# Projecting the queries of the last block by seven half-size products, in a kernel for gated attention with a mixture of experts

## The chip, the cores and the metric

The kernel runs on one core of a Trainium2 chip. The metric is the device time of one execution in microseconds (us), the median of several runs. A profile is one further execution, taken with the hardware profiler. The engines are TensorE (PE in the profile), VectorE (DVE), ScalarE (ACT), GpSimd (POOL) and SyncE (SP, which only issues transfers). PEld is TensorE's loading of weights. ACT, POOL and SP issue transfers (DMAs) from their own queues of instructions, in order: a transfer that must wait holds what is behind it on that engine.

## The reference

Two sequences of 2048 tokens, 512 wide, all in float32:

```
xn = layernorm(x)
z  = layernorm(xn) * gamma + beta
q, k, v = z @ qkv[:, :512], z @ qkv[:, 512:1024], z @ qkv[:, 1024:]
s  = softmax(causal(q @ k.T / sqrt(512))) @ v @ o_proj + xn
# mixture of experts on xn: 8 experts of 352 hidden units, the best 2 of each token
scores = xn @ gate_w.T + gate_b + bias
comb   = softmax over the 2 best scores, spread over the experts
h = silu(einsum('td,ehd->teh', xn, w1) + b1)
y = einsum('teh,edh->ted', h, w2) + b2
g = silu(einsum('td,te->t', y, comb))          # summed over the experts
out = x + s * g
```

## The kernel before

The work has four stages. **Projection** (to about 247 us): the 32 tiles of 128 tokens form 8 blocks of 512. The query and key weights are folded into one matrix `wqk`, the value and output weights into `wvo`, so each block has only queries (`wqk` on the left, the block's normalised rows `kT` on the right) and values (`kT` on the left, `wvo` on the right) to be made; `kT` itself serves as keys. **Routing** runs beside the last part of it: ranks, positions and lists of tokens for each expert, mostly on VectorE. **Experts** follow (`up`, `turn_h`, `join_h`, `down` for each tile of 128 sorted tokens), and then **attention**, with the gating and the output.

A block's queries are either four *units* (a unit is four products of 128x128 by 128x512, gathered in one PSUM bank, then copied by ScalarE and stored) or the seven products of the Strassen-Winograd scheme, each of four 128x128 by 128x256 products. `one_product(i, k)` makes product `k` of `items[i]`, where an item is a block's queries or its values. It needs sums of the weights (`wsums`, made once) and of the block's keys (`ksums`, by `key_sums`). The products 1, 2, 3, 4, 6 and 7 gather in the banks a, b and c; ScalarE copies bank_a into bank_b after product 1 and bank_b into bank_c after product 6, so that the later products add to what is there. Product 5 has bank_d and is added to two of the four results by VectorE, later: `with_fifth` puts the addition into `deferred`, and `add_due` emits it. Finished results go to `unstored`, and `store` issues their transfers; from block `LATE` = 5 on these stand on ScalarE's queue.

`SEVEN` = 7: the blocks 0 to 6 are made by seven products, the last block, 7, by eight units. `chain_of_products` gives the order of products, with two units of block 7 (the entries `None`) in the last item. `pieces` is a generator that yields after about every 7/4 products, or after a unit; the rest of the units follow at its end. The main loop, and then `route`, pull pieces and put other work between them; the order of the program is the order on each engine, as it is written out by hand. `route` emits its arithmetic between pieces; after its last `yield` come the list of tokens `toki`, six gathers on GpSimd, and the rest of the arithmetic (`ge`, `b1sel`, `share`). The last six pieces are pulled by the loop over `experts_step(-5)` to `experts_step(-1)`.

The memory is shared over time. `arena` holds the sums in six `areas` during the projection (area 0 the query weights' sums, 1 the value weights', 2 to 4 the sums of keys in turn, 5 a result) and later the second weights of the experts, `w2`, 1536 columns each, so that the experts 0 and 1 lie over area 0 and half of area 1, and 2 and 3 over the rest of 1 and area 2. `load_w2(e)` loads one expert's, in the order of `w2_left`. The pool `kp` has four buffers, in turn for the blocks' `kT` and, late, for results (`late_outs`). When the projection is over, its pools are closed, and `keep` (a mask, filled by GpSimd) and `w1s` (sums of the first weights, made by VectorE) take their memory.

Of the kernel before, what the change touches and what calls it, by code (L numbers as in the profile page):

```python
# [10 lines left out]
F32 = mybir.dt.float32  # L11
# [4 lines left out]
ALU = mybir.AluOpType  # L16
# [4 lines left out]
P = 128  # L21
# [5 lines left out]
def gated_attention_moe(  # L27
# [28 lines left out]
    nc = tc.nc  # L56
    B, S, D = x.shape
    E, _, H = w1_t.shape
# [6 lines left out]
    ND = D // P  # L65
# [79 lines left out]
    kp = right(stage_a, name="kp", bufs=BT)  # L145
# [54 lines left out]
    raw = w1p.tile([P, E * ND * H], F32, name="raw", tag="w1")  # L200
# [191 lines left out]
    def add_due(wait=2):  # L392
        while deferred and deferred[0][0] + wait <= made[0]:
            _, f, args = deferred.pop(0)
            f(*args)
# [40 lines left out]
            ratio.rearrange("p t o -> p o t").to_broadcast([P, E, BT]), ALU.mult,  # L436
        )

    def unit(b, u):

        kT = kts[b]
        po = banks[(u + 3) % ND]
        r = u % ND
        for c in range(ND):
            if u < ND:
                nc.tensor.matmul(
                    po, lhsT=wqk[:, c, ts(r, P)], rhs=kT[:, c, :],
                    start=(c == 0), stop=(c == ND - 1),
                )
            else:  # L450
                nc.tensor.matmul(
                    po, lhsT=kT[:, c, ts(r, P)], rhs=wvo[:, c, :],
                    start=(c == 0), stop=(c == ND - 1),
                )
        o = stg.tile([P, TB], F32, name=f"j_{b}_{u}", tag="stg")
        nc.scalar.copy(o, po)
        nc.scalar.dma_start(out=(qt_d if u < ND else v_d)[b][:, r, :], in_=o)
# [12 lines left out]
    def four(i):  # L470
        return areas[i].rearrange("p (k c d) -> p k c d", k=4, c=ND // 2)
# [3 lines left out]
        wsums[name] = four("qv".index(name))  # L475
        lhs_sums(wsums[name], w)

    def key_sums(b):

        assert all(k != b for _, _, _, k in pending)  # L480
        s = ksums[b] = four(2 + b % 3)
        b11, b12, b21, b22 = (
            kts[b][:, 2 * i : 2 * i + 2, ts(j, HD)] for i in range(2) for j in range(2)
        )
        nc.gpsimd.tensor_tensor(s[:, 0], b12, b11, ALU.subtract)
        nc.gpsimd.tensor_tensor(s[:, 1], b22, s[:, 0], ALU.subtract)
        nc.gpsimd.tensor_tensor(s[:, 2], b22, b12, ALU.subtract)
        nc.gpsimd.tensor_tensor(s[:, 3], b21, s[:, 1], ALU.subtract)

    items = [(b, of_q) for b in range(SEVEN) for of_q in (True, False)]
    FIFTH = {}

    def chain_of_products():
        yield from ((0, k) for k in (1, 5, 2, 6))
        for i in range(len(items) - 1):
            for j, k in (1, 1), (0, 3), (0, 7), (1, 5), (0, 4), (1, 2), (1, 6):
                yield i + j, k  # L500
        for k in (None, 3, 7, None, 4):
            yield len(items) - 1, k

    def one_product(i, k):

        b, of_q = items[i]
        w, s, t = wqk if of_q else wvo, wsums["q" if of_q else "v"], ksums.get(b)
        a11, a12, a21, a22 = (w[:, 2 * j : 2 * j + 2, ts(i, HD)] for i in range(2) for j in range(2))
        b11, b12, b21, b22 = (
            kts[b][:, 2 * i : 2 * i + 2, ts(j, HD)] for i in range(2) for j in range(2)  # L510
        )
        if k == 2 and i in (first_late, first_late + 2):
            late_outs.append(kp.tile([P, ND * D], F32, name=f"so_{i}", tag="kT"))
        outs = (
            raw[:, ts(i % NRAW, ND * D)] if i < first_late
            else areas[5] if i == first_late + 1
            else late_outs[int(i == first_late + 2)] if k in (2, 3, 7, 4) else raw[:, : ND * D]
        ).rearrange("p (g r d) -> p g r d", g=2, r=2)
        bank_a, bank_b, bank_c, bank_d = banks

        def multiply(bank, x, y, start=False):
            ps = bank.rearrange("p (r d) -> p r d", r=2)
            lhs, rhs = (x, y) if of_q else (y, x)
            for r in range(2):
                for c in range(2):
                    nc.tensor.matmul(
                        ps[:, r, :], lhsT=lhs[:, c, ts(r, P)], rhs=rhs[:, c, :],
                        start=(start and r + c == 0), stop=(c == 1), skip_group_check=True,
                    )

        def place(i, j):
            g, c = (i, j) if of_q else (j, i)
            return outs[:, g, :, ts(c, HD)]

        def whole(bank):
            return bank.rearrange("p (r d) -> p r d", r=2)

        def with_fifth(out, bank):
            nc.scalar.copy(out, whole(bank))
            deferred.append((made[0], nc.vector.tensor_tensor, (out, out, whole(FIFTH[i]), ALU.add)))  # L540

        if k == 1:
            multiply(bank_a, a11, b11, start=True)
            if i == 0:
                nc.scalar.copy(bank_b, bank_a)
        elif k == 5:
            multiply(bank_d, s[:, 0], t[:, 0], start=True)
            FIFTH[i] = stg.tile([P, TB], F32, name=f"p5_{i}", tag="stg")
            nc.scalar.copy(FIFTH[i], bank_d)
        elif k == 2:  # L550
            multiply(bank_a, a12, b21)
            nc.scalar.copy(place(0, 0), whole(bank_a))
        elif k == 6:
            multiply(bank_b, s[:, 1], t[:, 1])
            nc.scalar.copy(bank_c, bank_b)
        elif k == 3:
            multiply(bank_b, s[:, 3], b22)
            with_fifth(place(0, 1), bank_b)
            if i + 1 < len(items):
                nc.scalar.copy(bank_b, bank_a)  # L560
            while unstored:
                store(*unstored.pop(0))
        elif k == 7:
            multiply(bank_c, s[:, 2], t[:, 2])
            with_fifth(place(1, 1), bank_c)
            del FIFTH[i]
        else:
            multiply(bank_c, a22, t[:, 3])
            nc.scalar.copy(place(1, 0), whole(bank_c))
            queue = nc.sync if b < LATE else nc.scalar  # L570
            unstored.extend(((qt_d if of_q else v_d)[b], g, outs[:, g], queue) for g in range(2))

    def store(dst, g, src, queue):

        queue.dma_start(out=dst[:, 2 * g : 2 * g + 2, :], in_=src)
# [3 lines left out]
    def route():  # L579

        with ExitStack() as rt:
# [209 lines left out]
            nc.vector.tensor_copy(toki, tokf)  # L791
            for i in range(FIRST):
                gather(i)


            GS = [P, NJ, E]
# [113 lines left out]
    def pieces():  # L910

        n = 0
        for i, k in chain_of_products():
            if k is None:
                unit(*units.pop(next(j for j, (b, _) in enumerate(units) if b == SEVEN)))
                yield
                continue
            made[0] = n
            add_due()
            one_product(i, k)  # L920
            scale_next()
            n += 1
            if n * 4 // 7 > (n - 1) * 4 // 7:
                units.pop(0)
                yield
        while units:
            add_due(0)
            unit(*units.pop(0))
            while unstored:
                store(*unstored.pop(0))  # L930
            yield

    def sum_keys(i):
# [20 lines left out]
    def load_w2(e):  # L954
        nc.sync.dma_start(
            out=w2[:, e, : NH - 1, :],
            in_=w2_t[e, :full_rows, :].rearrange("(c p) d -> p c d", p=P),
        )
        nc.sync.dma_start(out=w2[:HL, e, NH - 1, :], in_=w2_t[e, full_rows:, :])
        nc.sync.dma_start(out=w2[HL : HL + 1, e, NH - 1, :], in_=b2[e : e + 1, :])  # L960
# [7 lines left out]
    def gather(i):  # L968
        xs = xsp.tile([P, ZW], U16, name=f"xs_{i}", tag="xs")
        nc.gpsimd.indirect_dma_start(  # L970
            out=xs, out_offset=None, in_=zu_d,
            in_offset=bass.IndirectOffsetOnAxis(ap=toki[:, order[i] : order[i] + 1], axis=0),
        )
        xss[i] = xs

    w2_left = [4, 5, 6, 7, 0, 1, 2, 3]
    done = LAST
    W2_FROM = 2 * ND * (SEVEN - 1) + 4
    for n in route():
        for _ in range(n):  # L980
            next(projected)
            done += 1
            for f, args in between.pop(done, []):
                f(*args)
            sum_keys(done)
            if done >= W2_FROM:
                load_w2(w2_left.pop(0))


# [407 lines left out]
    for i in range(-5, 0):  # L1397
        experts_step(i)
        for _ in range(min(2, len(units) - 1) if i < -1 else len(units)):
            next(projected)  # L1400
            if w2_left:
                load_w2(w2_left.pop(0))
    while w2_left:
        load_w2(w2_left.pop(0))
    stage_a.close()
    yp = st.enter_context(tc.tile_pool(name="yp", bufs=2))
    sm = right(att, name="sm2", bufs=4)
# [533 lines left out]
```

## Time and profile before

| what | value |
|---|---|
| time, median of 3 runs | 1008.62 us (1008.32 to 1014.06) |
| the profiled execution | 1007.83 us, span 1006.0 us |
| granted TensorE clock | 1.00 |
| instructions | 13431 |
| DMA | 207.96 MB, mean 207 GB/s |

The span is from the first to the last instruction of the profiled execution; the execution's time has a little more around it. In rows of the timeline the columns are: start, duration (both us), engine, line of the kernel, operation, output and inputs, shapes, how often, and in brackets the engine's idle time before it and what ended it. `ACTq` or `SPq` is an engine's queue that issues a transfer; its duration includes what it waited for. In the list of waits: who waited, for whom, us in total, how often, the longest. TensorE works on float32 in two passes, so a product of 128x128 by 128x512 is two rows of `128x512`. Rows of PE have an end that is modelled and overlaps the next start; the distance from start to start is the time that one takes.

### The profile page before, as it was taken

How to read it: one execution, taken by the hardware profiler on the slowest of the kernel's cores; microseconds unless marked ns; L12 is line 12 of the kernel's file. 1: busy time of each engine (PE TensorE's matmuls, PEld its weight loads, DVE VectorE, ACT ScalarE, POOL GpSimd, SP SyncE). 2: the span in 40 equal slices, each digit the busy share in tenths (PEclk: the TensorE clock that was granted, in tenths of full speed). 3: DMA queues.
4: the chain of work that ended last, by engine and by line, in shares of the span. 5: the costliest groups of instructions: out<-in, count | busy, mean ns of one | idle time of the engine just before them, and what ended most of it. 6: DMA issues, size and time to landing. Idle time of an engine off the chain costs nothing. (4 is left out here: it accounts for less than half of the span.)

```text
span 1006.0 us, 13431 instructions
## 1 busy us (share of the span) xinstructions
PE 999.9 (99%) x3924; PEld 665.3 (66%) x3924; DVE 716.9 (71%) x1396; ACT 403.2 (40%) x804; POOL 483.3 (48%) x475
## 2 busy tenths in 40 slices
PE   9999999999999999999999999999999999999998
PEld 5888888874567767766753448677675544447577
DVE  6996746897887777677744579668576556878667
ACT  3344445322444454444445112232335535442241
POOL 4474564004644454444332165254557776764272
PEclk9999999999999999999999999999999999999999
DMA  8689996978999999999999576274677768753361
GB/s 293 193 264 293 329 286 258 349 249 240 202 227 220 211 208 221 217 200 222 216 218 242 164 193 147 78 206 104 183 199 239 225 200 240 207 141 86 92 165 42
DMA packets 296647, 207.96 MB, mean 207 GB/s; under 512 B 230776, under 2 KB 243832, under 8 KB 296576
## 3 DMA queue, kind: packets, MB, share of 16 engines
q1 hardware_dynamic: 282432, 163.56, 63.2%
q0 software_dynamic: 10400, 34.63, 12.5%
q10 hardware_dynamic: 3744, 8.91, 2.4%
q8 instruction: 34, 0.56, 0.2%
q14 instruction: 37, 0.30, 0.1%
HBM read 92.35 MB, written 60.03 MB: 151 GB/s over the span
## 5 line engine op out<-in xcount | busy, mean ns | idle before, releaser
L1195 PE MATMUL py<-arena,ht 128*128 (+3 forms) x396 | 176.7, 593 | 0.0
L1307 PE MATMUL ps<-k,q 128*128 128x512 f32 (+3 forms) x416 | 143.0, 495 | 0.3 <-PEq L1455 0.3
L1495 POOL COPY pu<-pT 128x1024 uint16<-128x1024 uint16 (+2 forms) x74 | 82.5, 1146 | 118.1 <-ACT pT L1485 59.1
L1166 POOL COPY hu<-h 128x704 uint16<-128x704 uint16 x66 | 61.9, 956 | 155.8 <-issue 121.7
L1195 PEld LDWEIGHTS py<-arena,ht 128*128 128x128 f32 (+3 forms) x396 | 71.8, 185 | 80.7 <-issue 76.9
L1307 PEld LDWEIGHTS ps<-k,q 128*128 128x128 f32 x416 | 74.7, 190 | 67.1 <-issue 56.5
L970 POOL DMA_INDIRECT xs<-zu_d,toki x66 | 77.6, 1176 | 70.2 <-DVE toki L791 55.6
L1181 ACT ACTIVATE ht<-ht,b1sel 128x128 f32<-128x128 f32 (+3 forms) x216 | 67.9, 380 | 88.1 <-DVE ht L1175 88.1
L1145 DVE TENSOR_TENSOR h<-p,h 128x176 f32<-128x176 f32 x182 | 55.5, 337 | 60.7 <-PE p L1138 57.2
L1678 POOL DMA_INDIRECT yg<-y_d,posi x64 | 67.4, 1053 | 36.9 <-DVE yg L1689 21.9
L1535 PE MATMUL po<-v,pT 128*128 128x512 f32 x152 | 67.9, 592 | 0.0
L347 POOL COPY zu<-z 128x1024 uint16<-128x1024 uint16 x32 | 39.9, 1245 | 55.7 <-DVE z L332 55.7
L1517 DVE COPY pT<-puT 128x1024 uint16<-128x1024 uint16 (+2 forms) x74 | 54.1, 759 | 8.8 <-DMA puT<-pu 8.6
L1485 ACT ACTIVATE pT<-pT,nm 128x1024 f32<-128x1024 f32 x14 | 16.1, 1148 | 110.3 <-DVE nm L1395 72.0
L1203 ACT COPY y<-py 128x512 f32<-128x512 f32 x55 | 32.2, 585 | 62.3 <-PE py L1195 48.4
L1485 ACT ACTIVATE pT<-ps,nm 128x512 f32<-128x512 f32 (+3 forms) x52 | 30.1, 581 | 62.5 <-DVE nm L1395 38.8
L1365 DVE TENSOR_TENSOR pT<-p,pT 128x512 f32<-128x512 f32 x49 | 32.9, 687 | 25.8 <-PE p L1359 22.1
L1535 PEld LDWEIGHTS po<-v,pT 128*128 128x128 f32 x152 | 28.6, 190 | 31.9 <-issue 30.1
L1707 POOL TENSOR_TENSOR o<-o,yg 128x512 f32<-128x512 f32 x30 | 42.0, 1398 | 14.3 <-DVE o L1699 14.1
L1699 DVE SCALAR_TENSOR_TENSOR o<-xo,xscale,o 128x512 f32<-128x512 f32 x30 | 25.9, 871 | 30.1 <-ACT o L1696 30.1
L1046 DVE COPY xT<-xhT 128x1024 uint16<-128x1024 uint16 x66 | 45.2, 712 | 2.3 <-DMA xhT<-xs 2.0
L1708 POOL TENSOR_TENSOR o<-o,xo 128x512 f32<-128x512 f32 x30 | 43.0, 1432 | 2.4
(342 smaller groups left out, 2142.9 us busy)
## 6 DMA issues: line engine op xcount, KB each, us to landing
y_d<-y SPq DMA_DIRECT2D x66, 256.0 KB, 4.4
zu_d<-zu SPq DMA_DIRECT2D x32, 264.0 KB, 2.8
kt_d<-kT SPq DMA_DIRECT2D x16, 512.0 KB, 5.9
q<-qt_d SPq DMA_DIRECT2D x32, 256.0 KB, 5.4
k<-kt_d SPq DMA_DIRECT2D x32, 256.0 KB, 4.7
v<-v_d SPq DMA_DIRECT2D x32, 256.0 KB, 5.6
xo<-in_x_dram SPq DMA_DIRECT2D x32, 256.0 KB, 3.8
x<-in_x_dram SPq DMA_DIRECT2D x30, 256.0 KB, 4.9
```

Of the source, the lines that this page charges most:

```text
L970: nc.gpsimd.indirect_dma_start(out=xs, out_offset=None, in_=zu_d, in_offset=bass.IndirectOffsetOnAxis(ap=toki[:, order[i] : order[i] + 1], ...
L1046: nc.vector.tensor_copy(xT.bitcast(U16).rearrange("p c (t h) -> p c t h", h=2), xhs.pop(i).rearrange("p (h c) t -> p c t h", h=2),)
L1145: nc.vector.tensor_tensor(out, x, y, ALU.add)
L1166: nc.gpsimd.tensor_copy(hu[:, :, :H], h.bitcast(U16).rearrange("p (d h) -> p h d", h=2))
L1181: nc.scalar.activation(ht[:hn, c, at], ht[:hn, c, at], AF.Silu, bias=b1sel[:hn, c, j : j + 1])
L1195: nc.tensor.matmul(py[at, :], lhsT=ht[:k, c, at], rhs=rhs[n], start=(c == 0), stop=(c == NH - 1),)
L1307: nc.tensor.matmul(ps[:, :w], lhsT=aqs[seq[s] // 2][:, c, ts(t % 2, P)], rhs=aks[first + j][:, c, :w], start=(c == 0), stop=(c == ND - 1),)
L1485: nc.scalar.activation(turned[s][:, at:end], src, AF.Exp, bias=nm, accum_out=rs[:, j : j + 1])
L1495: nc.gpsimd.tensor_copy(pu[:, : 2 * w].rearrange("p (h d) -> p h d", h=2), turned[s][:, k : k + w].bitcast(U16).rearrange("p (d h) -> p h ...
L1517: nc.vector.tensor_copy(turned[s][:, k : k + w].bitcast(U16).rearrange("p (i t h) -> p i t h", t=P, h=2), puT[:, : 2 * w // P, :].rearrang ...
L1535: nc.tensor.matmul(dst, lhsT=turned[s][:, ts(k, P)], rhs=avs[first + k // BT][:, k % BT, cols], start=(start and k == k0), stop=(k == k1 - 1),
L1678: nc.gpsimd.indirect_dma_start(out=y, out_offset=None, in_=y_d, in_offset=bass.IndirectOffsetOnAxis(ap=posi[k][:, n : n + 1], axis=0),)
```

## The change

Block 7's queries are made by seven half-size products, as item `CHAINED` = 14. The two units inside the chain are now its value units 4 and 5; after the chain come unit 6, products 1 and 5, product 6, unit 7 (into bank_d), products 3 and 7, products 2 and 4, in six steps as before. The results of products 2, 3, 4 and 7 lie in `late_outs[1]`, a buffer of `kp` that held block 6's queries. The key sums of block 7 are made by VectorE (the others by GpSimd) in a fresh buffer of `kp`, right after the first gathers are issued. As the query weights' sums in area 0 are now needed to the end, the second weights of the experts 2 and 3 are loaded where those of 0 and 1 were, and 1 and 0 after the last step.

```diff
-    def unit(b, u):
+    def unit(b, u, po=None):
         kT = kts[b]
-        po = banks[(u + 3) % ND]
+        po = banks[(u + 3) % ND] if po is None else po
...
-    def key_sums(b):
+    def key_sums(b, at=None, engine=nc.gpsimd):
-        s = ksums[b] = four(2 + b % 3)
+        s = ksums[b] = four(2 + b % 3) if at is None else at
...
-        nc.gpsimd.tensor_tensor(s[:, 0], b12, b11, ALU.subtract)
+        engine.tensor_tensor(s[:, 0], b12, b11, ALU.subtract)
...
     items = [(b, of_q) for b in range(SEVEN) for of_q in (True, False)]
+    CHAINED = len(items)
+    items.append((SEVEN, True))
...
-            else late_outs[int(i == first_late + 2)] if k in (2, 3, 7, 4) else raw[:, : ND * D]
+            else late_outs[int(i in (first_late + 2, CHAINED))] if k in (2, 3, 7, 4) else raw[:, : ND * D]
...
         if k == 1:
             multiply(bank_a, a11, b11, start=True)
-            if i == 0:
+            if i in (0, CHAINED):
                 nc.scalar.copy(bank_b, bank_a)
...
             for i in range(FIRST):
                 gather(i)
+            last = kp.tile([P, ND * D], F32, name="last_sums", tag="kT")
+            key_sums(SEVEN, last.rearrange("p (k c d) -> p k c d", k=4, c=ND // 2), nc.vector)
...
             if k is None:
-                unit(*units.pop(next(j for j, (b, _) in enumerate(units) if b == SEVEN)))
+                unit(*units.pop(next(j for j, at in enumerate(units) if at >= (SEVEN, ND))))
...
-        while units:
+        for step in (2 * ND - 2,), (-1, -5), (-6,), (2 * ND - 1,), (-3, -7), (-2, -4):
             add_due(0)
-            unit(*units.pop(0))
+            for u in step:
+                if u > 0:
+                    unit(SEVEN, u, banks[3] if u == 2 * ND - 1 else None)
+                else:
+                    one_product(CHAINED, -u)
+            add_due(0 if step[-1] == -4 else 1)
             while unstored:
                 store(*unstored.pop(0))
+            units.pop(0)
             yield
...
-    w2_left = [4, 5, 6, 7, 0, 1, 2, 3]
+    w2_left, w2_last = [4, 5, 6, 7, 2, 3], [1, 0]
...
-            if done >= W2_FROM:
+            if done >= W2_FROM and w2_left:
                 load_w2(w2_left.pop(0))
...
             next(projected)
-            if w2_left:
-                load_w2(w2_left.pop(0))
-    while w2_left:
-        load_w2(w2_left.pop(0))
+    for e in w2_left + w2_last:
+        load_w2(e)
```

More of the change, by code (lines that the diff above doesn't have):

```diff
@@ L484, in key_sums @@
         )
-        nc.gpsimd.tensor_tensor(s[:, 0], b12, b11, ALU.subtract)
-        nc.gpsimd.tensor_tensor(s[:, 1], b22, s[:, 0], ALU.subtract)
-        nc.gpsimd.tensor_tensor(s[:, 2], b22, b12, ALU.subtract)
-        nc.gpsimd.tensor_tensor(s[:, 3], b21, s[:, 1], ALU.subtract)
+        engine.tensor_tensor(s[:, 0], b12, b11, ALU.subtract)
+        engine.tensor_tensor(s[:, 1], b22, s[:, 0], ALU.subtract)
+        engine.tensor_tensor(s[:, 2], b22, b12, ALU.subtract)
+        engine.tensor_tensor(s[:, 3], b21, s[:, 1], ALU.subtract)
     items = [(b, of_q) for b in range(SEVEN) for of_q in (True, False)]
+    CHAINED = len(items)
+    items.append((SEVEN, True))
     FIFTH = {}
@@ L497, in chain_of_products @@
         yield from ((0, k) for k in (1, 5, 2, 6))
-        for i in range(len(items) - 1):
+        for i in range(CHAINED - 1):
             for j, k in (1, 1), (0, 3), (0, 7), (1, 5), (0, 4), (1, 2), (1, 6):
@@ L501, in chain_of_products @@
         for k in (None, 3, 7, None, 4):
-            yield len(items) - 1, k
+            yield CHAINED - 1, k
     def one_product(i, k):
@@ L558, in one_product @@
             with_fifth(place(0, 1), bank_b)
-            if i + 1 < len(items):
+            if i + 1 < CHAINED:
                 nc.scalar.copy(bank_b, bank_a)
```

## The prediction

> **What bounds the kernel now.** I read the page's shares, then the list of waits for PE (the chain of waits, which reaches back to 568 us only, doesn't cover this stage), then the timelines of PE, ACT, DVE and POOL around 225 to 257 us, where the last block is projected and the first experts begin.
>
> ```profile
> PE 999.9 (99%) x3924; PEld 665.3 (66%) x3924; DVE 716.9 (71%) x1396; ACT 403.2 (40%) x804; POOL 483.3 (48%) x475
> ...
> PE warm L870 <- DVE b1s L181: 1.1, 1, 1.1
> PE p L1583 <- DVE u L1600: 0.4, 1, 0.4
> PE ps L1307 <- PEq L1455: 0.3, 1, 0.3
> ```
>
> PE is busy all the time, and its waits come to 2 us in all: PE work removed is time won, and any wait of PE is time lost. The projection's tail on PE, then ACT, DVE and POOL:
>
> ```profile
> 224.54 1.94 PE L526 MATMUL bank_c<-wvo,arena 128*128 128x256 f32 x8
> 226.32 3.60 PE L446 MATMUL bank_b<-kT,wqk 128*128 128x512 f32 x8
> 229.76 3.60 PE L446 MATMUL bank_c<-kT,wqk 128*128 128x512 f32 x8
> ...
> 243.49 3.60 PE L451 MATMUL bank_c<-wvo,kT 128*128 128x512 f32 x8
> 246.92 9.63 PE L1086 MATMUL ph<-w,xT 128*128 x32
> ...
> 229.96 0.59 ACT L456 COPY j<-bank_b 128x512 f32<-128x512 f32 x1 [1.31 <-PE bank_b L446]
> 230.57 0.34 ACTq L457 DMA_DIRECT2D qt_d<-j  x1
> 230.95 9.05 ACTq L575 DMA_DIRECT2D v_d<-so  x2
> 240.05 0.59 ACT L456 COPY j<-bank_c 128x512 f32<-128x512 f32 x1 [9.51 <-DVE so L395]
> ...
> 225.34 0.20 DVE L791 CAST toki<-tokf 128x68 int32<-128x68 f32 x1
> 238.97 0.68 DVE L395 TENSOR_TENSOR so<-so,p 128x512 f32<-128x512 f32 x1
> ...
> 247.15 0.20 POOL L1414 MEMSET keep<- 128x128 f32 x1 [6.00 <-PE bank_c L451]
> 250.16 0.81 POOL L1166 COPY hu<-h 128x704 uint16<-128x704 uint16 x1 [0.38 <-ACT h L1164]
> ...
> ACT j L456 <- DVE so L395: 9.5, 1, 9.5
> PEld py L1195 <- ACT ht L1181: 0.5, 2, 0.2
> ```
>
> The row to look at is ACT at 230.95. ACT issues the two stores of block 6's values; the second needs DVE's add of 238.97 (the fifth product, `add_due`), which stands on DVE behind all the routing arithmetic. For 9 us ACT does nothing else. Today that costs nothing: the units rotate over four banks, each starts anew in its bank, and PE needs none of the copies behind the stores until bank_c at 243.49, 2.9 us after that bank's copy ended at 240.64.
>
> **The change, part by part.**
>
> *Products.* From 226.32 six units of 3.43 us (229.76 less 226.32) follow: 20.6 us. After it there are two units and seven half-size products of 1.73 us (206.52 to 208.25 on PE): 6.9 + 12.1 = 19.0 us. **Gain 1.6 us**, all of it on PE. The value units 4 and 5 that take the places of query units 0 and 1 cost the same; unit 7 in bank_d finds it free. ACT gets seven copies of 0.59 us for four, DVE two adds of 0.68 us, and two stores of 512 KB replace four of 256 KB; ACT (40% busy) and DVE hide these, but for the places below.
>
> *Key sums on DVE.* Four subtractions of 128x512, between `toki` (225.54) and the routing's rest. Nearest row: the same shape at L239, 0.69 us and then 0.60 from start to start, four in 2.5 us (39.65 to 42.19). Four others of that line, at 33.3 to 37.5 us, took 0.68, 1.53, 0.68 and 1.52: two ran beside POOL's copies. The Trainium skill (SBUF — State Buffer, "SBUF: two separate sides") says that DVE with two SBUF inputs and a GpSimd operation that reads SBUF lock each other out for whole instructions. POOL issues six gathers from 225.8 to 234.2; by the rule, if they hold the lock, all four sums take 1.5 us: 6 us. The row says otherwise: DVE's two-input steps beside those gathers (L804, 128x608) stayed at 0.79 us, as their like (L824) did after the gathers. I take 2.5 us; 6 is the upper end. The sums themselves are in time: the first is done at 226.2, the fifth product uses it at 231.5. The tile takes block 6's key buffer, which PE leaves at about 218. But all that follows on DVE comes 2.5 us later, and so does the add: 241.5 to 242.2.
>
> *The wait it adds.* Product 6 accumulates in bank_b on a copy of product 1 that **ACT** writes there (`nc.scalar.copy(bank_b, bank_a)`). The first of the new steps is unit 6, followed at once by the stores of block 6's values, so this copy stands behind the blocked store. PE: unit 6 ends at 229.76, product 1 at 231.5, product 5 at 233.2; product 6 could start there. ACT: the add ends at 242.2, 0.4 us later (as from 239.65 to 240.05) the copy starts, 0.57 us later it is done: 243.2. **PE waits 10.0 us** (bounds: 7.5 if the sums cost DVE no time, 13.5 with sums of 6 us; that it doesn't wait at all is the first rival). Behind product 6 on PE's queue is everything else.
>
> *The clock after such a wait.* The skill (TensorE: Matmul & The Clock Gate, "What's actually happening") says that an idle window of 3.4 us halves the array's clock until a busy one has passed. After the start the trace has no PE wait over 0.4 us, so it can't show this. At the start the granted clock reads 1.00 from the first microsecond, yet the warm-up's twelve passes of 128 columns took 2.93 us, 0.24 each, where transposes of that width later took 0.13; full pace came at about 5 us. So the granted clock doesn't show it, but the durations do. By the granted clock alone the price is 0; by the start and the rule it is half of some 3.8 us. I take **1.9 us**; bounds 0 and 3.4.
>
> PE then has product 6, unit 7 and four products left: 1.7 + 3.4 + 6.9 = 12.1 us, with the cold clock 14.0. The first expert (`up`, 246.92 before) starts at 257.2.
>
> *What comes free later.* `keep` and `w1s` lie where the projection's key buffers were. Today they wait for PE's last product (POOL at 247.15, 0.2 us after PE). The block's query outputs will lie in one of these buffers (`late_outs[1]`) and be stored from it last: PE ends at 257.2, the copy of product 4 at 258.0, the stores are issued one after the other, the second at 258.4. Landing for such stores was 3.1 to 8.4 us in this trace, median 4.3 (I take it, as SP's late weights load at the same time): 262.7, that is 5.5 us after `up` starts. POOL is in order: from `keep` to the earliest start of the first `hu` are 2.7 us (fill, select, gather of 1.45). So `hu` starts 8.3 us after `up` begins, not 3.2 as before. The first `down` was just in time behind that chain (the last row above: PE's weight load waited for ACT's `ht`), so it is late by **4.9 us** (bounds 2.5 and 9, with landing at 3.1 and 8.4). DVE's `w1s` waits as long and holds the third tile's join; that is inside the same 4.9.
>
> *Second weights.* Experts 2 and 3 load where 0 and 1 did, 1 and 0 behind the last step. SP waits with them until product 7 has read the query sums, about 3.5 us before PE's end, and then issues six transfers (0.3 to 0.5 us each); behind them stand the fifth tile's transpose and the first `huT`. Cover: `down` needs these weights some 14 us after `up` begins. I put it at nothing; without cover, up to 3 us.
>
> **Sum:** -1.6 + 10.0 + 1.9 + 4.9 = +15.2 us. Profiled span 1006.0 to 1021.2, its execution 1007.83 to 1023.0. The median of the runs shown, 1008.62, is 0.8 above that execution: **1023.8 us**, 1.5% slower. About 1% is what a measurement of this kernel tells from no change.
>
> **Rivals.**
> 1. *The gain arrives (faster by the 1.6 us, 1007.0).* The copy of product 1 isn't held. This decides if block 6's last add is done before about 232 us. For it: that bank copy is new and the trace can't show its wait. Against: ACT's idle 9.5 us until that very add, and the routing's rest still stands ahead of it. 0.05; with the late stores alone, 1011.9: 0.06.
> 2. *Only the first wait costs* (`hu` and `down` not held, or stores landing within 3 us): 1008.6 - 1.6 + 10.0 + 1.9 = 1018.9, without a cold clock 1017.0. For it: stores of 2.6 us at 204 us, when DMA was quiet. 0.16.
> 3. *Worse:* the sums are locked out by gathers (+3.4) or landing takes 8.4 us (+4): 1027 to 1031. 0.07.
>
> My case has 0.66, with 1019.5 to 1027. The range 1016 to 1028 leaves out rival 1 and most of 3. Slower by over 1% (above 1018.7): 0.66, half of rival 2 and rival 3, 0.80; within 1%: 0.18; faster by more than 1%: 0.02, as no part removes 10 us.
>
> **What would show it.** After: ACT held at `v_d<-so` until about 242; PE's list of waits led by bank_b at L526 on ACT, about 10 us; passes of 256 columns at twice their pace just after it; `keep` and `w1s` released by the DMA `qt_d<-so`, 5 to 6 us after PE's last product; a wait of PE at L1086 or L1195 of about 5 us in all. Wrong if PE runs through from 226 to 246 us, if the add comes ahead of the routing's rest, or if `keep` starts right behind PE.

## The result, and the profile after

| | before | after |
|---|---|---|
| median of 6 runs each | 1008.06 us (1007.47 to 1014.06) | 1026.25 us (1024.64 to 1026.88) |
| the profiled execution | 1007.83 us, span 1006.0 us | 1026.05 us, span 1024.3 us |
| granted TensorE clock | 1.00 | 0.991 |

The change makes the kernel slower: ratio 1.0171, interval 1.0155 to 1.0188. The first answer is in the page's shares and the list of PE's waits, in which the first two rows are new.

```profile
PE 1004.1 (98%) x3948; PEld 672.9 (66%) x3948; DVE 723.5 (71%) x1402; ACT 404.5 (39%) x807; POOL 482.4 (47%) x475
```

```profile
PE bank_b L528 <- ACT bank_b L547: 9.8, 1, 9.8
PE ph L1096 <- DVE xT L1056: 4.1, 1, 4.1
PE warm L874 <- DVE b1s L181: 1.1, 1, 1.1
PE p L1591 <- DVE u L1608: 0.5, 1, 0.5
```

PE's busy time rose by 4.2 us although it has less arithmetic to do. So the waits are not all of it, and some of the work ran slower. The timeline of PE, from the first of the new steps to the first `down`, shows where:

```profile
226.76 3.60 PE L451 MATMUL bank_b<-wvo,kT 128*128 128x512 f32 x8
230.20 1.89 PE L528 MATMUL bank_a<-kT,wqk 128*128 128x256 f32 x8
231.92 1.89 PE L528 MATMUL bank_d<-last_sums,arena 128*128 128x256 f32 x8
243.57 3.78 PE L528 MATMUL bank_b<-last_sums,arena 128*128 128x256 f32 x8 [9.76 <-ACT bank_b L547]
247.14 4.17 PE L451 MATMUL bank_d<-wvo,kT 128*128 128x512 f32 x8
251.15 1.89 PE L528 MATMUL bank_b<-kT,arena 128*128 128x256 f32 x8
...
258.05 4.90 PE L1096 MATMUL ph<-w,xT 128*128 x16
267.06 7.51 PE L1096 MATMUL ph<-w,xT 128*128 x16 [4.11 <-DVE xT L1056]
274.42 1.88 PE L1205 MATMUL py<-arena,ht 128*128 x4
```

Product 6 (at 243.57) takes 3.57 us from start to start, where products 1 and 5 take 1.73; unit 7 takes 4.01 instead of 3.43; the two `up` from 267.06 take 7.36 instead of 4.74. Each slow stretch stands directly behind a wait. The whole loss can be read off these starts:

| stretch | before | after | of the difference |
|---|---|---|---|
| start of the first new step | 226.32 | 226.76 | +0.44 |
| from there to `up` | 20.60 | 31.29 | +9.76 wait, +2.42 slow (243.57 to 251.15 is 7.58, against 5.16), -1.49 work |
| from `up` to `down` | 9.47 | 16.37 | +4.11 wait, +2.62 slow, +0.17 |
| start of `down` | 256.39 | 274.42 | +18.03 |

The executions are 18.2 us apart: all but the 0.44 us at the start arises in these 48 us. The table adds up PE's own time; what the second slow clock is worth by itself is taken up below.

The windows of the after kernel, five us each, show the slow stretches as granted clock. After the window and its length stand the busy time and count of PE, PEld, DVE, ACT and POOL; the last three columns are granted clock, DMA share and GB/s.

```profile
235.00:240.00 5.00, 0.00 (x0) 0.00 (x0) 4.79 (x7) 0.00 (x0) 0.00 (x0) 0.80 1.24 245
240.00:245.00 5.00, 1.43 (x3) 1.17 (x4) 3.05 (x7) 1.07 (x2) 1.33 (x8) 0.50 1.00 222
245.00:250.00 5.00, 5.00 (x12) 3.07 (x11) 0.00 (x0) 0.57 (x1) 0.00 (x0) 0.67 0.12 49
...
265.00:270.00 5.00, 2.94 (x5) 1.85 (x6) 4.97 (x6) 0.00 (x0) 4.63 (x5) 0.53 0.36 87
```

What released the two waits stands in the timelines of ACT, DVE and POOL:

```profile
231.38 11.53 ACTq L577 DMA_DIRECT2D v_d<-so  x2
242.95 0.57 ACT L547 COPY bank_b<-bank_a 128x512 f32<-128x512 f32 x1 [11.97 <-DVE so L395]
...
258.33 0.86 ACTq L577 DMA_DIRECT2D qt_d<-so  x2
...
273.30 0.99 ACT L1191 ACTIVATE ht<-ht,b1sel 128x128 f32<-128x128 f32 x3 [8.46 <-DVE ht L1185]
```

```profile
241.86 0.68 DVE L395 TENSOR_TENSOR so<-so,p 128x512 f32<-128x512 f32 x1
...
264.59 0.89 DVE L1118 TENSOR_TENSOR w1s<-w 128x704 f32<-128x704 f32 x1 [7.87 <-DMA qt_d<-so]
...
266.32 0.69 DVE L1056 COPY xT<-xhT 128x1024 uint16<-128x1024 uint16 x1
...
269.30 3.49 DVE L1118 TENSOR_TENSOR w1s<-w 128x704 f32<-128x704 f32 x1
272.71 0.55 DVE L1185 COPY ht<-huT 128x768 uint16<-128x768 uint16 x1
```

```profile
264.68 0.20 POOL L1422 MEMSET keep<- 128x128 f32 x1 [21.02 <-DMA qt_d<-so]
...
267.25 0.78 POOL L1176 COPY hu<-h 128x704 uint16<-128x704 uint16 x1
...
269.66 1.67 POOL L1118 TENSOR_TENSOR w1s<-w 128x704 f32<-128x704 f32 x1
271.27 0.77 POOL L1176 COPY hu<-h 128x704 uint16<-128x704 uint16 x1
```

ACT sits in the queue row at 231.38 until DVE's add of 241.86, and only then makes the bank copy that product 6 needs. 22 us later `keep` and `w1s` both start when the query stores have landed (264.6), and the join `xT` that the third `up` needs stands behind two of the `w1s` sums on DVE.

A second path to `down` is nearly as late as PE's: `keep` holds the gather and `hu` (267.25) on POOL, and `ht`, which `down` reads, begins only at 273.30. The transposed `hu` had landed by 270.9, but DVE's copy of it stands behind a `w1s` sum of 3.49 us, where such a sum alone takes 0.88: this one ends 0.75 us after GpSimd's own sum and copy beside it (272.04).

### The profile page after: what moved, and what is told of

It is laid out like the page before. It is cut to its first block, busy times and chain, and to the rows that moved or that the text cites. A ratio compares the mean times of both kernels' runs of the same rounds, so it can differ in the third digit from the quotient of the medians.

```text
span 1024.3 us, 13481 instructions
## 1 busy us (share of the span) xinstructions
PE 1004.1 (98%) x3948; PEld 672.9 (66%) x3948; DVE 723.5 (71%) x1402; ACT 404.5 (39%) x807; POOL 482.4 (47%) x475
```

## The experiments

The theory: ACT held behind block 6's addition (9.8), the stores' hold on the freed memory (4.1) and the slow clock behind each make the loss. The rival that grew during the study: something else in the change, first of all the later loads of the second weights, takes the gain even where these waits are gone. The edits below are against the kernel after, but for the sums alone and the weights alone, which are against the kernel before. All ratios are to the kernel before on the same chip.

### The first wait: the addition early

```diff
             key_sums(SEVEN, last.rearrange("p (k c d) -> p k c d", k=4, c=ND // 2), nc.vector)
+            add_due(0)
```

> The last outstanding addition of block 6's values (what the store on ScalarE's queue waits for) is emitted right behind the new key sums, ahead of the routing's rest; nothing else differs from the changed kernel. If the held store is what keeps PE from product 6: ACT is free by about 230 us, PE's wait on bank_b (9.8 us) falls under 0.5 us, the slow clock behind it (2.4 us) goes with it, and the time is 1026.2 - 12.2 = 1014. The wait before the third up (4.1 us) and its slow clock stay. If PE instead waits for the key sums on VectorE, or a full wait comes up elsewhere in the tail: 1022 to 1026.

Measured: 1019.06 us (1017.34 to 1020.58), ratio 1.0099 (1.0078 to 1.0119). The wait at bank_b fell from 9.8 to 0.6, so the held copy is shown to be its cause. But only 7 of some 12 us came back, as the second wait grew to 10.2 us. The waits of PE, and then the timeline of ACT:

```profile
PE ph L1097 <- DVE xT L1057: 10.2, 1, 10.2
...
PE bank_b L528 <- ACT bank_b L547: 0.6, 1, 0.6
```

```profile
246.81 7.49 ACTq L577 DMA_DIRECT2D qt_d<-so  x2
254.50 1.00 ACT L1175 ACTIVATE h<-ph,xs 128x352 f32<-128x352 f32 x2 [7.18 <-DMA arena<-in_b_dram]
```

Nothing in the computation ties a query store to an expert's weights, and yet the row puts its release down to the landing of such a load. The trace names the counter that each transfer updates when it lands: those of SP and ACT share eight, and in the traces of the kernels before and after a transfer on one of them goes out, with few exceptions, only when all sixteen landings of the one before it are counted. Here the second query store has the counter of expert 1's first load: SP issued that load at 246.96, its last part landed at 253.87, and the store went out at 253.97. (The bias that the row names is only the nearest landing.) In the kernel after, the load on that counter had landed by 256.85, before the store's turn at 258.86, since PE was so late.

### Other orders of the steps

The query products first, the value units 6 and 7 last, in a single run:

```diff
-        for step in (2 * ND - 2,), (-1, -5), (-6,), (2 * ND - 1,), (-3, -7), (-2, -4):
+        for step in (-1, -5), (-6,), (-3, -7), (-2, -4), (2 * ND - 2,), (2 * ND - 1,):
```

> Only the order of the six last steps differs from the changed kernel: the seven query products first, value units 6 and 7 last. If keep and w1s wait for the stores of block 7's queries: these stores now land under the two units, keep starts within 1 us of PE's last product, and the wait before the third up (4.1 us) and its slow clock (2.6 us) are gone. The held store stays: it now stands ahead of the copy of bank_b to bank_c, so PE waits some 11 us for product 3. Time 1020. If the second wait comes from the late loads of the experts' weights or from the gathers, it stays: 1026 or more.

Measured: 1022.22 us, clock 0.993. The first wait is 11.5 us (now at bank_b for the copy into bank_c), the second only 0.7 (at `up`, for `keep`): with the query stores two units earlier their landing is hidden (PE's last product releases `keep`, not a store), and no slow clock follows in the experts.

Both edits together:

> The early addition and the values last together. If the two waits are separate and each has the cause named: no PE wait over 2 us is left in the tail. The additions of the new item's own fifth product still stand behind the routing's rest, so that its stores go out at about 243 us and land at about 247.5, some 2 us after PE's last product: 0 to 2 us may be left at the first experts. Time 1006.5 to 1008.5, against 1008.1 before. If one wait hid another cause: 1012 or more.

Measured: 1018.26 us (1016.48 to 1019.52), ratio 1.0089 (1.0072 to 1.0106): a miss. The wait at bank_b is 0.7, but two waits at `up` of 3.1 and 4.6 us stand in its place. The last copy for the query stores began at 239.52, but their additions stand on DVE behind the routing's rest and end at 243.26; ACT issued the first store at 244.56, when a transpose on its counter had landed (244.47), and the second behind a weights load on its own (landed 247.32). The copy that follows them waited 7.68 us.

### The clock: PE kept busy through the wait

Ten products of 128x512 into a spare bank between products 5 and 6; nobody reads them.

```diff
             add_due(0)
+            if step == (-6,):
+                warm_st = ExitStack()
+                spare = psum(warm_st, name="ps_w", bufs=1).tile([P, TB], F32, name="spare")
+                for _ in range(10):
+                    nc.tensor.matmul(spare, lhsT=wqk[:, 0, :P], rhs=wqk[:, 0, :], start=True, stop=True)
+                warm_st.close()
             for u in step:
```

> The changed kernel with ten products of 128x128 by 128x512 into a spare bank, read by nothing, between products 5 and 6 (8.6 us at full pace): the wait for the copy is as long, but PE isn't idle. If an idle PE loses its clock: the granted clock stays at 1.00 through 235 to 250 us, product 6 and unit 7 run at full pace, and the time falls by 2.4 us to 1023.8. If the slow products have another cause (banks, copies, power), or the fill costs what it saves: 1026 or more.

Measured: 1022.96 us (1021.35 to 1023.4), ratio 1.0143 (1.0126 to 1.016). PE's timeline:

```profile
233.06 8.75 PE L936 MATMUL spare<-wqk 128*128 128x512 f32 x20
243.01 1.99 PE L528 MATMUL bank_b<-last_sums,arena 128*128 128x256 f32 x8 [1.20 <-ACT bank_b L547]
244.84 3.60 PE L451 MATMUL bank_d<-wvo,kT 128*128 128x512 f32 x8
248.27 1.89 PE L528 MATMUL bank_b<-kT,arena 128*128 128x256 f32 x8
```

Product 6 starts at the same time as in the kernel after, within 0.6 us, and now takes 1.83 us instead of 3.57, unit 7 3.43 instead of 4.01. Useless work makes the kernel faster: the slow pace came from the idleness, not from contention or operands. The time fell by 3.3 us, 2.4 expected; the second wait was 2.9 instead of 4.1 here, which the fill doesn't explain.

### The sums alone

The kernel before with the key sums of block 7 on VectorE, in the place where the change has them; nobody reads them.

```diff
             for i in range(FIRST):
                 gather(i)
+            last = kp.tile([P, ND * D], F32, name="last_sums", tag="kT")
+            key_sums(SEVEN, last.rearrange("p (k c d) -> p k c d", k=4, c=ND // 2), nc.vector)
```

> The kernel before with only the key sums of block 7 on VectorE added, at the place that the change gives them; nothing reads them. Theory: they put the addition that the held store needs 2.5 us later (to about 242 us), and that is all; the copy of bank_c ends at 243.1 instead of 240.6, still just ahead of unit 7 at 243.5. So 1008.1 to 1008.5, no change; PE's waits in the tail under 0.5 us. If the sums lengthen the routing or the gathers, or PE needs the copies earlier: 1010 or more.

Measured: 1008.32 against 1007.96 us, ratio 0.9998 (0.9988 to 1.0008). By themselves the sums cost nothing. Their 2.5 us count only when PE waits for the add behind them.

### The second wait: weights from another queue

The weights of experts 1 and 0 from ACT's queue, behind the query stores, so that the stores come first (the new argument `queue` of `load_w2` isn't shown):

```diff
     for e in w2_left + w2_last:
-        load_w2(e)
+        load_w2(e, nc.scalar)
```

> The changed kernel with the second weights of the experts 1 and 0 loaded from ScalarE's queue, behind the stores of block 7's queries, instead of from SP's ahead of them. If keep and w1s wait for those stores, and the stores (5.5 us to landing) share the DMA engines with these loads: landing in 3.5 to 4.3 us, keep starts 1.2 to 2 us earlier, the wait before the third up falls from 4.1 to 2 to 3 us, and the time from 1026.2 to about 1024. The first down doesn't wait for the weights. If the second wait came from the late weights: down waits for them, 1026 to 1030.

Measured: 1024.54 us (1023.98 to 1025.37), ratio 1.0164 (1.0149 to 1.018), which doesn't part it from the kernel after. The second wait is 2.9 instead of 4.1 us: `keep` starts 5.3 us after `up` began, 6.6 in the kernel after. Together with the early addition:

> The early addition and the weights behind the stores together. With the early addition alone the second wait grew from 4.1 to 10.2 us, as ACT's second store of the queries stood 7.5 us for a transfer of weights that SP had issued late. If that is the cause: with the weights behind the stores ACT's two stores go out at once, land in 3.5 to 4.5 us, and the second wait is 2 to 4 us; no wait over 1 us at bank_b. Time 1026.2 - 12.2 - 1.5 = 1012.5, from 1019.1 with the early addition alone. If the stores are slow because the gathers and transposes have moved into them: the wait stays over 8 us and the time at 1018.

Measured: 1015.71 us (1012.73 to 1016.66), ratio 1.0069 (1.0053 to 1.0084). The wait at bank_b is 0.5, the second 6.9 instead of the 2 to 4 expected: the stores went out from 247.93 to 250.6, held by a transpose's counter, and the weights' issues behind them held ACT's first silu until 254.25.

### The second wait: nothing on the freed memory

`keep` is filled in the experts' fifth step (its lines move, not shown), and the sums `w1s` are spread over the fourth to seventh instead of the first to seventh:

```diff
-        for _ in range((2, 2, 1, 4, 3, 3, 1)[i] if 0 <= i < paired.start else 0):
+        for _ in range((0, 0, 0, 4, 4, 4, 4)[i] if 0 <= i < paired.start else 0):
```

> The changed kernel, with the work that takes the stored buffers' memory put later: keep is filled in the fifth expert step, and the sixteen sums into w1s are spread over the fourth to the seventh step instead of the first to the seventh. Stores, loads and the projection's order are untouched. If the second wait is keep and w1s waiting for the stores of block 7's queries: the wait before the third up (4.1 us) and its slow clock (2.6 us) are gone, hu is no later than before, and the wait at bank_b (9.8 us) stays. Time 1026.2 - 6.7 = 1019.5. If joins or down wait for the transfers themselves (transposes, gathers, weights): a wait over 2 us stays, 1023 to 1026.

Measured: 1023.19 us (1022.67 to 1025.28), ratio 1.0152 (1.0137 to 1.0168). PE's timeline has the four `up` without a wait and at full pace:

```profile
258.18 9.63 PE L1096 MATMUL ph<-w,xT 128*128 x32
267.64 2.74 PE L1205 MATMUL py<-arena,ht 128*128 x6
```

This shows the hold on `keep` and `w1s` to be the second wait's cause: `down` starts at 267.64 instead of 274.42. But only part of this is kept, and the time is 3.7 us above the 1019.5 expected: later products wait 2.4 and 1.1 us in the list of PE's waits. I put that down to the sums now crowded on DVE; the list doesn't name them.

### Where the gain went

Three kernels take the first wait away, or all but 0.7 us of it, and go against the second. The first has the addition early and the values last, and pulls four pieces of the projection ahead of parts of the routing's rest, so that their additions on DVE don't stand behind all of it:

```diff
             key_sums(SEVEN, last.rearrange("p (k c d) -> p k c d", k=4, c=ND // 2), nc.vector)
+            add_due(0)
+            yield 3
...
+            yield 1
             for c in range(NH):
                 nc.vector.tensor_tensor(
...
-        for step in (2 * ND - 2,), (-1, -5), (-6,), (2 * ND - 1,), (-3, -7), (-2, -4):
+        for step in (-1, -5), (-6,), (-3, -7), (-2, -4), (2 * ND - 2,), (2 * ND - 1,):
```

> The early addition, values last, and the last four query products pulled in the middle of the routing's rest, so that the additions of their own fifth product stand on VectorE ahead of the expert tables (b1sel) and not behind them, and the stores go out some 4 us earlier. If everything that the change lost lies in held stores: the stores go out by 242 to 245 us, ahead of the loads of weights, and land before or within 2 us of PE's last product at 245.7; no PE wait over 1 us in the tail, or one of 1 to 2 us at the third up; time 1006.5 to 1009. If transfers in the tail are short of DMA time whatever their order: stores landing after 250 us, and 1012 or more.

Measured: 1015.42 us (1014.01 to 1017.75), ratio 1.0082 (1.0068 to 1.0095). PE's waits:

```profile
PE ph L1099 <- DMA arena<-in_w_t_dram: 3.3, 1, 3.3
PE py L1208 <- ACT ht L1194: 1.7, 1, 1.7
PE ph L1099 <- DVE xT L1059: 1.7, 1, 1.7
```

A miss again: 6.7 us of waits in the experts, the longest put down to the landing of a weights load.

The second is the kernel with nothing on the freed memory, and besides it block 6's stores issued not at a step's end but with product 3 (`one_product` issues what is `unstored` there), so that product 1's copy stands ahead of them, and the last weights loaded behind the experts' first step (the move of `keep` and `w1s` isn't shown again):

```diff
-            while unstored:
+            while unstored and step[-1] == -4:
...
-    for e in w2_left + w2_last:
-        load_w2(e)
...
         experts_step(i)
+        if i == 0:
+            for e in w2_left + w2_last:
+                load_w2(e)
```

> As the run with keep and w1s put later, and two edits more. The stores of block 6's values aren't issued in the first of the new steps, but with product 3, when their addition is done, so that they don't hold the copy of bank_b and don't move into the gathers; and the loads of the experts 1 and 0 stand in the program behind the first expert step, so that no store waits for them. If the loss is made up of held instructions alone: no PE wait over 0.5 us in the tail, up starts at about 245.5 us (246.9 before), and the time is that of before less the 1.6 us of fewer products: 1006.0 to 1007.0 against 1008.0. If the transfers' crowding in the tail is a loss of its own: waits of some us before up or down, 1010 or more.

Measured: 1015.64 us (1014.73 to 1016.25), ratio 1.0072 (1.0059 to 1.0086). Its PE timeline:

```profile
227.09 3.60 PE L451 MATMUL bank_b<-wvo,kT 128*128 128x512 f32 x8
...
246.04 9.63 PE L1096 MATMUL ph<-w,xT 128*128 x32
262.01 4.82 PE L1205 MATMUL py<-arena,ht 128*128 x6 [6.34 <-DMA arena<-in_w_t_dram]
```

Here the change does what it is for: 18.95 us from the first new step to `up`, without a wait, where it was 20.60, and `up` starts 0.9 us earlier than in the kernel before. But the expected 1006 to 1007 was missed: `down` lacks its weights, 6.3 us, and its slow clock (4.66 us to the next start, against 2.58).

The third is this kernel with the last weights from ACT's queue behind the query stores, in their place of the change:

```diff
     for e in w2_left + w2_last:
-        load_w2(e)
+        load_w2(e, nc.scalar)
```

> The kernel that moves the addition's store, the half-matrices' memset and the weight sums out of the way (e11), with one thing different: the second weights of experts 1 and 0 are loaded from ACT's queue directly behind the two query stores, instead of from SP's queue behind a transpose of the MLP's second step. There ACT comes at 247.2 us, SP came at 251.4. My theory (what is left over the kernel before is the first down product's wait for those weights, 6.3 us, and the slow clock behind it, 2.1 us): the weights land some 4 us sooner, the wait falls to 2 to 3 us and the slow clock with it, so 1009.5 to 1012. Rival (the load is bound by the transfers it shares the DMA engines with, not by its issue): it lands at 261 to 262 again and the time stays at 1015 to 1016. Second rival (ACT's issues hold the first silu and with it the first hidden half): a wait for ht or at the first up of 2 to 3 us in its place, 1012 to 1015.

Measured: 1015.39 us (1014.82 to 1017.34), ratio 1.0074 (1.006 to 1.0088): no better. The weights are no longer what `down` waits for; the first row is PE's timeline, the second DVE's.

```profile
261.37 5.41 PE L1205 MATMUL py<-arena,ht 128*128 x6 [5.41 <-ACT ht L1191]
```

```profile
260.31 0.56 DVE L1185 COPY ht<-huT 128x768 uint16<-128x768 uint16 x1 [13.38 <-DMA huT<-hu]
```

SP issued that transpose `huT` at 253.17 and it arrived at 260.3, 7 us later; in the kernel before it took 3.9 us (251.00 to DVE's copy at 254.96). In the second of these kernels it took 4.2, so that 3.0 us are lost in it. Another 3.1 stand ahead of it: ACT's six issues of weights hold its first silu until 251.76 (248.66 in the second), and `hu` starts at 252.38 instead of 249.27, which is the second rival's hold. The loads had got out of SP's way and stood in ACT's, and the transpose met full DMA engines (share 1.21 from 255 to 260 us); that the loads slowed it is argued from this, not shown.

The last run asks for the weights' share by itself: the kernel before with the change's order of loads and nothing else.

```diff
-    w2_left = [4, 5, 6, 7, 0, 1, 2, 3]
+    w2_left, w2_last = [4, 5, 6, 7, 2, 3], [1, 0]
...
-            if w2_left:
-                load_w2(w2_left.pop(0))
-    while w2_left:
-        load_w2(w2_left.pop(0))
+    for e in w2_left + w2_last:
+        load_w2(e)
```

> The kernel before with the second weights' order of the change alone: those of experts 4, 5, 6, 7, 2, 3 with the chain's last pieces as before, and those of experts 1 and 0 loaded behind the last pieces instead of among them. Queries, values and key sums stay as they were. My theory (the last loads wait for nothing of their own; they only have to land before the first down product, 9.5 us after the first up): no change, 1007.5 to 1009.5. Rival (the two loads fall among the transposes and stores at the expert stage's start and land late, or hold a store by the counters that the queues share): the first down product waits 3 to 6 us, 1011 to 1015.

Measured: 1014.02 us (1013.76 to 1014.38), ratio 1.0058 (1.0043 to 1.0073). My theory fell: this edit, priced at nothing, costs 5.8 us by itself. PE's waits, then ACT's and POOL's rows behind them:

```profile
PE py L1195 <- ACT ht L1181: 2.9, 1, 2.9
PE ph L1086 <- DVE xT L1046: 1.2, 1, 1.2
```

```profile
252.75 0.59 ACT L456 COPY j<-bank_c 128x512 f32<-128x512 f32 x1 [5.79 <-DMA qt_d<-j]
```

```profile
250.58 0.20 POOL L1412 MEMSET keep<- 128x128 f32 x1 [9.37 <-DMA v_d<-j]
```

No instruction of the expert stage waits for the weights. ACT's copy of the last unit waits until a store has landed (252.75; before, the same copy began at 247.12), `keep` starts at 250.58 instead of 247.15, and `down` at 260.95 instead of 256.39, slow behind its wait. The windows of 245 to 250 us say why, in the kernel before and with the weights alone; the third is 255 to 260 us in the kernel after, where its loads are:

```profile
245.00:250.00 5.00, 5.00 (x16) 2.78 (x15) 2.84 (x4) 1.05 (x2) 2.40 (x3) 1.00 0.43 161
```

```profile
245.00:250.00 5.00, 5.00 (x17) 2.75 (x16) 0.00 (x0) 1.17 (x2) 0.00 (x0) 1.00 1.15 245
```

```profile
255.00:260.00 5.00, 5.00 (x22) 3.98 (x22) 1.30 (x2) 1.56 (x3) 0.00 (x0) 1.00 1.06 280
```

Before, gathers, transposes and stores fill the DMA engines up to 245 us (share 1.08 in the window ahead of it), and then there is air, 0.43. The two loads are 1412 KB (512, 192 and 2 KB each, twice); at the 297 GB/s of that full window this is an estimated 4.8 us of all DMA engines, and they take it where the stores and the first transposes of the experts have to land: the store that ACT's copy waits for took 8.9 us from its issue at 243.76 to its last landing, its like in the kernel before 4.8. The shared counters have a part too: that store and a later one stood 1.3 and 1.1 us until the loads on their counters had landed. How the 5.8 us split between the two no run shows.

In the kernel after, PE's wait has let the engines run empty (share 0.12 from 245 to 250 us, shown above): the loads of 253.07 to 255.6 find the older stores and transposes done and meet only the query stores (share 1.06). The change's own stall hid most of what the change costs otherwise.

## Why the prediction was right, and where its sum was not

It forecast 1023.8 us, slower, and the mechanism; 1026.25 was measured. The errors of its terms hardly cancel, so the sum didn't come near by luck. Only the second weights were cheap here for another reason than the one given. By its steps:

- **Products, -1.6.** -1.49 in the kernel after, -1.65 where nothing waits (18.95 against 20.60).
- **Key sums, 2.5 us taken.** 225.89 to 228.43, 2.54 us, 0.68 to 0.69 each, beside the gathers. The lock-out rule of the Trainium skill (SBUF — State Buffer, "SBUF: two separate sides"), 6 us, did not come into play beside gathers; the row did. It fits the second wait, which the prediction didn't try it on: `w1s` sums with two inputs, 0.88 us alone, took 1.85 and 3.49 beside GpSimd's copies and its own sum, and ended 0.74 and 0.75 us after these.
- **The wait for bank_b, 10.0.** 9.76, with the add at 241.86 (taken 241.5), the copy at 242.95. The early addition shows the cause by taking it away.
- **The slow clock behind it, 1.9.** 2.4, and the filled wait shows that it is one. The text inferred from the start that the granted clock wouldn't show it. Here the rows read 0.80, 0.50 and 0.67: it does. The start was no evidence, since the trace's records of the granted clock begin only at 5.00 us there, and the view gives 1.00 where it has none. The rule of the Trainium skill (TensorE: Matmul & The Clock Gate, "What's actually happening"), half the clock behind idleness, agrees with the 0.50; its 3.4 us are no threshold for a wait, as 2.9 us were enough in three kernels.
- **Later freed memory, 4.9: the term that was mis-sized.** The mechanism is as told: `keep` and `w1s` released by the query stores, and `down` late behind the chain over `hu`. But from `up` to `down` it measured 16.37 against 9.47 us, 6.9 in place of 4.9. `keep` started 6.6 us after `up` began (5.5 taken; the stores landed in 5.5 us, not 4.3). `hu` started at 9.2 (8.3 taken), and the first `ht` at 15.25 instead of 8.67: 6.6 later, as DVE's slow `w1s` sum held it. PE's own path was just as late: 4.1 us of wait at the third `up`, behind `w1s` and the join, and 2.6 of slow clock, which the sum didn't put behind this wait. The two don't add up. With the weights alone PE waited for `ht` and went on 0.45 us after it began (260.50, 260.95); here that would have been 273.75, so at full pace `down` would have come an estimated 0.7 us sooner, not 2.6.
- **What the sum left short.** It gave +15.2, and `down` started 18.0 later: +2.0 on the term above, +0.5 on the first slow clock, +0.44 on the start, +0.1 on the products, less 0.2 on the first wait. The 0.44 arises ahead of the new steps and stayed unexplained (0.77 in the kernel with 246.04).
- **Second weights at nothing.** Not quite nothing in the kernel after: behind the query stores they let these land sooner, and the time was 1.7 us lower, which the intervals don't part. Wrong as a price: "without cover, up to 3 us" was 5.8, through the DMA engines and the shared counters and not through SP's order, which is where the text looked. So the first rival's 1007.0 and 1011.9 were too low: of the kernels without the first wait none had a median below 1015.3.

No variant beats the kernel before. It stays open why the kernel that ran through to `up` (1015.6) is some 3 us above 1008.5 - 1.65 + 5.8 = 1012.7; the longer wait at `down` (6.3, against 1.2 and 2.9 with the weights alone) is where it shows, and there the loads go out only from 251.37 (239.42). Query sums elsewhere in memory, so that all weights could load as early as before, were not tried.

## What to carry to other kernels

When a new instruction takes a place on an in-order queue, look at what is waiting ahead of it there: ACT's nine idle us were free until a copy that PE needs stood behind them. Reckon with a slow clock behind each wait of PE of a few us, and then ask whether another path to the next product is as late anyway. And a transfer that "has time" still takes the DMA engines' time, and can hold a store whose counter it shares: before pricing a later load at nothing, read the DMA share of the windows that it moves into, and ask whether the air there exists without the change's own stall.

## What the runs showed of the hardware

- The slow clock's price hardly grows with the wait: 2.4 us behind 9.8, 2.6 behind 4.1, 2.0 behind 10.2 (the early addition), 1.9 behind 2.9 (the weights from ACT's queue). The traces record when the granted clock changed: each stretch at 0.50 behind a wait lasts 3.41, 6.83, 10.24 or 13.65 us, that is one to four times 3.41, and only the part of it in which PE works costs time (4.71 us of the 10.24 behind the first wait).
- The length of the wait alone doesn't decide. Behind 1.2 and 1.7 us there was no slow clock, and behind 2.9 us there was in three kernels. Behind the 3.3 us of the kernel with the additions between, the profiled execution's clock reads 1.00 throughout; of its five executions two read 1.00, two 0.998 and one 0.996.
- Transfers of two queues that share completion counters can hold each other without any dependency between their data: ACT stood 7.2 us for a load of SP (the early addition).
- VectorE's sums of two inputs from SBUF, 0.88 us alone, took 1.85 and 3.49 beside GpSimd's copies and sum; beside its gathers, sums of 128x512 stayed at 0.68 to 0.69.
- A transpose of 1.2 us on its queue took 7 us to arrive where the DMA share was 0.98 and then 1.21 (the third of the kernels under "Where the gain went"), 3.9 where it was 0.71 (before).
